# A graph attention layer on one core: ScalarE fetches rows of one tile in every 16th pair, issues the sum loads, and the last stores lose their order

## The chip, the core and the metric

The kernel runs on one core of a Trainium2 chip. The core has a matrix engine (PE in the profile; PEld are its weight loads), a vector engine (DVE), a scalar engine (ACT, called ScalarE in the text), a general engine (POOL) and a sync engine (SP) that mostly issues transfers. Each engine works through its own queue in order, and semaphores tie the queues together. Transfers run on 16 DMA engines which all queues share. SP, ScalarE and POOL can issue them; rows marked SPq, ACTq or POOLq are what these queues do themselves. The metric is device microseconds for one execution, less is better.

## The reference

A pre-norm graph layer over 12,500 nodes of 128 features and 400,000 edges that are sorted by destination (`dst`), with 32 attributes each:

```python
h = jnp.maximum(_layernorm(x, axis=-1), 0.0)
# inside the layer, on hn = ln1(h):
src = jnp.concatenate([edge_index[0], loop]); dst = jnp.concatenate([edge_index[1], loop])
ea = jnp.concatenate([edge_attr, mean of edge_attr for each self loop])
x_l = (hn @ W_l).reshape(n, H, C); x_r = (hn @ W_r).reshape(n, H, C); e = (ea @ W_e).reshape(-1, H, C)
m = jax.nn.leaky_relu(x_l[src] + x_r[dst] + e, 0.2)
alpha = jnp.einsum('ehc,hc->eh', m, att)
a = softmax of alpha over the edges of each dst
out = jax.ops.segment_sum(x_l[src] * a[:, :, None], dst, num_segments=n)
h2 = h + out + bias
result = x + h2 + gelu(ln2(h2) @ W1 + b1) @ W2 + b2
```

(The self-loop and softmax lines are told in words; H is 8 heads, C 16 features of a head, n the number of nodes.)

## The kernel before

**Start.** Nodes are padded to 98 tiles of 128. The start normalises them in quads of four tiles, multiplies by `W_l` and stores rows of 136 floats (128 products, then eight ones, which sum the weights later) in `xl_dram`; all of that must be stored before a row can be gathered from it. Meanwhile POOL gathers raw inputs for 29 pairs (`raw_gather`, L339), whose rows are later computed in the kernel instead of being gathered. Near the end of the start, at step 14, SP loads the table `hand_sb` (L841): for each tile whose rows are fetched one by one, the 128 source indices of its edges, one partition for a tile. In memory these indices lie apart, so the transfer has 4 bytes an element. At step 16 DVE multiplies them by the row size (L851), in the middle of its work on the quads.

**Pairs and rounds.** The edges form 3125 tiles of 128; four tiles are a pair (two units of two tiles), and there are 782 pairs, the last with one tile. One long loop, unrolled and ordered by hand, runs over rounds r. In each round a table of stages is gone through in order, each for the pair c = r minus its delay, and this order is the order of every engine's queue:

- `gather` (delay -4, L1078): POOL fetches each tile's 128 rows of `xl_dram` by one indirect DMA into `xs`, which has 12 buffers
- `combine` (0): PE transposes the four tiles of rows (L1143) and adds the products of destination rows and edge attributes (L1146)
- `slope` and `bend` (1): ScalarE scales (L1157), DVE takes the maximum (L1162)
- `apart`, `score` (2): PE multiplies by the attention weights (L1152, L1167)
- `lowest` (3): DVE takes minima (L1173); `weigh` (3): ScalarE's two exponentials (L1184)
- `turn` (4): PE transposes the weights (L1192); `keep_turned` (5): ScalarE copies them (L1197)
- `collect` (6): PE multiplies weights by rows (L1206); `own_heads` (7): DVE picks each head's part (L1215, L1221) into the record `rec`
- `put` (8, a late stage): SP stores the record in the `state` tensor (L1230)
- `windows` (-4, late, every fourth round): SP loads attributes, destinations and destination rows for four pairs (L1104 to L1119)

Each stage waits for stages of an earlier round on another engine, and for the `lowest`/`weigh` and `slope`/`bend` pairs in the same round. Within a round ScalarE's order is `keep_turned`, `slope`, `weigh`, then whatever else falls in the round: square roots and normalisations of node groups, which need other activation tables than the exponential (rows ACT_TABLE_LOAD).

**Rows fetched one by one.** In some pairs the fourth tile isn't gathered by POOL. `hand` issues 128 transfers of one row (544 bytes) each instead, L1056, spread over the rounds ahead, and every 16 rows it loads 16 row addresses from `hand_sb` into registers (`words`, L1010). There are two `ways`: SP does 35 pairs, from 30 in steps of 22 (last 778); ScalarE does 11 pairs, from 77 in steps of 64 (last 717), two rows a round, issued behind all other work of the round. One round before the pair comes up, the queue waits until all 128 rows have landed. The tiles have two buffers for each way.

**Stores.** The records of different pairs lie apart, so `put` may lift the order among its stores, but it does so only where `fetched` (the list of rows that SP issued in this round) isn't empty. SP issues rows up to round 771, so from pair 764 on each store waits until the one before has landed. `put` also reads the stores' addresses, four at a time (`ats`, from `at_sb`, L1010), in the round where `windows` needs them first.

**Mean of the attributes.** `sum_load` (L1248) loads 98 pieces of 512 KB, one every second round in rounds 0 to 194, on SP's queue; DVE sums them.

**Node groups.** When a group of nodes has all its records, its two states are loaded (`f_state`, L1292) and merged, normalised and passed through the feed-forward part in steps with a round each. The second last group's steps are the table `soon`, from round 774 on; the last group's (`last_steps`) come behind the last pair, in round 790 and 791, and end the kernel with the store of its output (L1545).

Of the kernel before, what the change touches and what calls it, by code (L numbers as in the profile page):

```python
# [22 lines left out]
P = 128  # L23
# [14 lines left out]
QP = 4  # L38
# [24 lines left out]
BEHIND = 3  # L63
# [9 lines left out]
HAND_LEAD = 6  # L73
HAND_READ = 16
LANDED = 7
BESIDE_EVERY = 64
BESIDE_FIRST = 77
BESIDE_LANDED = 3
# [874 lines left out]
def window_edges(  # L953
# [30 lines left out]
    with ExitStack() as es:  # L984
# [51 lines left out]

        def hand(r, w):

            w["new"].clear()
            hands, n = w["pairs"], w["sems"]  # L1040
            i, k = divmod(r + HAND_LEAD + hands.step - hands[0], hands.step)
            if k == HAND_LEAD - 1 and 0 < i <= len(hands):
                all_here = w["queue"].wait_ge(w["landed"][(i - 1) % n], ((i - 1) // n + 1) * P * 16)
                tc.declare_fence(all_here.ins, group=f"{w['name']}{i - 1}")
            if not 0 <= i < len(hands):
                return
            d = by_hand[hands[i]]
            if k == 0:
                d["x"] = once.tile([P, XW], F32, name=f"{w['name']}{i % 2}")
            for e in range(P * k // hands.step, P * (k + 1) // hands.step):  # L1050
                if e % HAND_READ == 0:
                    d["at"] = words(
                        hand_sb[w["at"] + i : w["at"] + i + 1, e : min(e + HAND_READ, P)], (NT * P - 1) * XW * 4,
                        w["engine"],
                    )
                row = w["queue"].dma_start(  # L1056
                    d["x"][e : e + 1, :].bitcast(U8), rows_at(xl_dram, d["at"][e % HAND_READ], 1, XW * 4)
                )
                row.then_inc(w["landed"][i % n], 16)
                tc.no_tile_sem_insts.add(row.ins.name)  # L1060
                tc.add_to_no_dep_group(f"{w['name']}{i}", row.ins)
                w["new"].append(row)
# [162 lines left out]
        def put(c):  # L1225
            if c % QP == 0:
                for i in range(c, min(c + QP, n_pr)):
                    pairs[i]["put"] = ats(c // QP + BEHIND)[1 + i - c]
            d, nu = pairs[c], len(tiles_of(c))
            store = nc.sync.dma_start(states_at(d["put"])[:, 0:nu], d["rec"][0 : KN * H, 0:nu].bitcast(U8))  # L1230
            if fetched:
                tc.declare_no_dep(
# [3 lines left out]
            tc.add_to_no_dep_group("states", store.ins)  # L1236
            if fetched:
                tc.declare_no_dep(
                    store.ins, group="merged",
                    reason="pairs behind a node group's round begin above its nodes, which the check of destinations asks",  # L1240
                )


        sums = [None] * NL

        def sum_load(i):
            sums[i] = fin.tile([P, LW], F32, name="ea_s", tag="big", bufs=3)
            nc.sync.dma_start(  # L1248
                sums[i],
# [294 lines left out]
        def f_put(d):  # L1544
# [15 lines left out]
            (-1, place),  # L1560
        )
        late_stages = (
            (-WAHEAD, windows),
# [43 lines left out]
            (1, f_low),  # L1607
            (2, f_exp),
            (3, f_den),
            (4, f_out),  # L1610
            (5, f_h),
            (6, f_stats),
            (7, f_root),
            (8, f_scale),
            (8, f_rest),
        )
# [63 lines left out]
        with tc.manual_schedule():  # L1680
            for r in range(-AHEAD, max(last_round, groups[-1]["round"] + 18)):
                in_round(r, early, groups[:-2])
                for late, f in stages:
                    c = r - late
                    if 0 <= c < n_pr:
                        f(c)
                for late, f in sum_stages:
                    i, off = divmod(r - late, SUM_STEP)
# [9 lines left out]
                in_round(r, enumerate(raw_steps), raw)  # L1698
                for w in ways:
                    hand(r, w)  # L1700
                t, off = divmod(r, CLEAR)
# [363 lines left out]
```

## Time and profile before

| | before |
|---|---|
| median of 3 runs | 3902.61 us (3902.32 to 3906.65) |
| profiled execution, its own time | 3904.92 us |
| span of the profiled execution | 3903.2 us |
| PE busy | 3414.5 us (87%) |
| POOL busy | 2913.6 us (75%), of it 2798.4 in 2963 gathers |
| DVE busy | 2799.8 us (72%) |
| ACT busy | 2177.5 us (56%) |
| rows fetched by SP, by ScalarE | 4480, 1408 |
| DMA traffic | 549.30 MB, 141 GB/s on the mean |

How to read a profile row: a group has its line in the kernel, its engine and operation, what it writes and reads, and how often; then busy time, mean duration in ns, and the idle time of the engine just ahead of it with what ended that idle time ("<-"). "issue" means that the engine waited for nothing that the profile shows. Timeline rows begin with the start and the duration in us, chain rows (the chain of work that ended last) likewise. Window rows have the busy time and number of instructions of PE, PEld, DVE, ACT and POOL in a stretch, then the clock granted to PE, the busy share of the DMA engines and GB/s. Rows of one line's instructions have minimum/median/maximum duration in ns, then first and last start. A query's rows are not quoted with their headings.

### The profile page before, as it was taken

Reading aid. Unit: us, or ns where it says so; the run is one execution under the profiler, and the core shown is the slowest. Engines: PE = TensorE matmul, PEld = TensorE weight load, DVE = VectorE, ACT = ScalarE, POOL = GpSimd, SP = SyncE. Lnnn points to the kernel's source line nnn. Section 1 sums busy time; section 2 is a strip of 40 time slices with the busy share of each in tenths; the row PEclk is TensorE's granted clock in tenths of the full one; section 3 lists DMA queues with packets and bytes.
Section 4 is the critical chain, followed back from the end, with each engine's and each line's share of the span. In section 5 each row is a group of like instructions: output and inputs, shape, how many; then the busy total and the mean of one; then the engine's idle time right before and its main releaser. Section 6 shows DMA issues by size and latency. Waiting matters only on the chain.

```text
span 3903.2 us, 70516 instructions
## 1 busy us (share of the span) xinstructions
PE 3414.5 (87%) x18461; PEld 2329.9 (60%) x18463; DVE 2799.8 (72%) x6142; ACT 2177.5 (56%) x4745; POOL 2913.6 (75%) x3092
## 2 busy tenths in 40 slices
PE   3588899889899989998999899999998989898988
PEld 3356566556566666665666666666666666666655
DVE  5577877777776776777777777777777767667665
ACT  6545555555565555555555555655555556456444
POOL 7777777777777777777777777777777777777773
PEclk6799999999999999999999999999999999999999
DMA  8767777777766666665565555555565555555553
GB/s 203 236 163 173 184 184 182 177 185 185 177 135 134 136 131 130 137 132 125 123 131 124 123 126 126 125 123 121 121 125 126 123 123 112 124 122 117 122 119 65
DMA packets 546765, 549.30 MB, mean 141 GB/s; under 512 B 248891, under 2 KB 425372, under 8 KB 545932
## 3 DMA queue, kind: packets, MB, share of 16 engines
q1 hardware_dynamic: 444290, 329.68, 34.3%
q0 software_dynamic: 98528, 214.12, 28.9%
q8 instruction: 150, 2.46, 0.3%
q14 instruction: 261, 2.14, 0.2%
q10 hardware_dynamic: 3536, 0.91, 0.1%
HBM read 482.08 MB, written 62.28 MB: 139 GB/s over the span
## 4 chain that ended last, share of the span: by engine, by line
PE 36%; POOL 24%; DMA 20%; issue 13%; DVE 2%; SPq 1%; ACT 0%; ACTq 0%; POOLq 0%
POOL xs L1078 24%; DMA xs<-xl_dram,src_sb 19%; PE z L1146 8%; PE acc L1206 8%; PE ab L1167 6%; PE pt_ps L1192 4%; PE z L1143 4%; PE ab L1152 2%; PE acc L1525 1%; DMA state<-rec 0%; DVE rec L1173 0%; PE acc L1500 0%; PE pt_ps L759 0%; DMA zw<-xr_dram 0%; PE acc L1328 0%
## 5 line engine op out<-in xcount | busy, mean ns | idle before, releaser
L1078 POOL DMA_INDIRECT xs<-xl_dram,src_sb x2963 | 2798.4, 944 | 904.3 <-issue 783.9
L1184 ACT ACTIVATE p<-ab,rec 128x256 f32<-128x256 f32 x1563 | 656.4, 471 | 923.6 <-DVE rec L1173 909.3
L1215 DVE TENSOR_TENSOR own<-acc,diag 128x272 f32<-128x272 f32 x782 | 342.6, 438 | 821.9 <-PE acc L1206 813.2
L1143 PE MATMUL z<-ident,xs 128*128 128x128 f32 x3079 | 564.7, 283 | 360.6 <-DMA xs<-xl_dram,src_sb 337.9
L1206 PE MATMUL acc<-xs,pt 128*128 128x136 f32 x6158 | 873.7, 286 | 0.0
L1143 PEld LDWEIGHTS z<-ident,xs 128*128 128x128 f32 x3079 | 395.3, 142 | 776.8 <-DMA xs<-xl_dram,src_sb 449.7
L1146 PE MATMUL z<-ea,zw 128*128 128x512 f32 x1564 | 828.0, 612 | 6.5 <-DMA xs<-xl_dram,src_sb 6.5
L1197 ACT COPY pt<-pt_ps 128x512 f32<-128x512 f32 x782 | 456.2, 583 | 643.6 <-PE pt_ps L1192 585.5
L1167 PE MATMUL ab<-m,negrep 128*128 128x512 f32 x1564 | 806.4, 597 | 0.2 <-issue 0.2
L1206 PEld LDWEIGHTS acc<-xs,pt 128*128 128x128 f32 x6158 | 800.7, 197 | 0.0
L1192 PEld LDWEIGHTS pt_ps<-ident,p 128*128 128x128 f32 x3125 | 408.0, 146 | 345.0 <-issue 269.7
L1162 DVE TENSOR_TENSOR m<-z,zs 128x512 f32<-128x512 f32 x782 | 533.6, 682 | 108.1 <-ACT zs L1157 106.2
L1129 DVE TENSOR_SCALAR ea<-dl,wid 96x516 f32<-96x516 bf16 x782 | 575.4, 736 | 8.0 <-DMA dl<-dc_dram 8.0
L1173 DVE TENSOR_REDUCE rec<-ab 128x2 f32<-128x512 f32 x781 | 539.0, 690 | 14.2 <-PE ab L1167 13.7
L1192 PE MATMUL pt_ps<-ident,p 128*128 128x128 f32 x3125 | 490.7, 281 | 0.6 <-ACT p L1184 0.6
L1157 ACT ACTIVATE zs<-z 128x512 f32<-128x512 f32 x782 | 471.8, 603 | 31.0 <-PE z L1146 31.0
L1221 DVE TENSOR_REDUCE rec<-own 128x34 f32<-128x272 f32 x782 | 340.9, 436 | 26.7
L1152 PE MATMUL ab<-ne,farw 128*128 128x512 bf16 (+1 forms) x781 | 306.8, 393 | 24.6 <-ACT p L1184 22.9
L1146 PEld LDWEIGHTS z<-ea,zw 128*128 128x128 f32 x1564 | 253.1, 202 | 7.3 <-issue 6.8
L1167 PEld LDWEIGHTS ab<-m,negrep 128*128 128x128 f32 x1564 | 245.8, 195 | 1.1 <-DMA ea_s<-in_ea_t 0.7
L1152 PEld LDWEIGHTS <-farw 128*128 128x128 bf16 x782 | 78.1, 100 | 211.9 <-issue 102.2
L1184 ACT ACT_TABLE_LOAD x102 | 130.9, 1283 | 1.8
(249 smaller groups left out, 2215.6 us busy)
## 6 DMA issues: line engine op xcount, KB each, us to landing
dl<-dc_dram SPq DMA_DIRECT2D x196, 396.0 KB
hand<-xl_dram SPq DMA_DIRECT2D x4480, 0.5 KB
ea<-in_ea_t SPq DMA_DIRECT2D x196, 256.0 KB
ea_s<-in_ea_t SPq DMA_DIRECT2D x98, 512.0 KB
xs<-xl_dram,src_sb POOLq DMA_INDIRECT x2963
beside<-xl_dram ACTq DMA_DIRECT2D x1408, 0.5 KB
state<-empty SPq DMA_DIRECT2D x98, 144.0 KB
f_st<-state SPq DMA_DIRECT2D x46, 288.0 KB
```

The lines of the kernel that those rows point to most:

```text
L1078: nc.gpsimd.indirect_dma_start(out=xs[:, j, :], out_offset=None, in_=xl_dram, in_offset=bass.IndirectOffsetOnAxis(ap=src_sb[:, c * KP + j ...
L1129: nc.vector.tensor_scalar(d["ea"][0:WN].rearrange("p (a b) -> p a b", b=OW), d["dl"][0:WN].rearrange("p (a b) -> p a b", b=OS)[:, :, 0:OW] ...
L1143: nc.tensor.matmul(z[:, j * P : (j + 1) * P], row_of(c, j)[:, 0:P], ident, start=(j == 0), stop=False, is_transpose=True)
L1146: nc.tensor.matmul(z[:, :e], d["zw"], d["ea"][:, :e], start=False, stop=True)
L1152: nc.tensor.matmul(d["ab"][:, :e], d["far"], d["ne"][:, :e], start=True, stop=False)
L1157: nc.scalar.activation(d["zs"][:, :e], d["z"][:, :e], AF.Copy, scale=SLOPE)
L1162: nc.vector.tensor_tensor(d["m"][:, :e], d["z"][:, :e], d["zs"][:, :e], op=OP.max)
L1167: nc.tensor.matmul(d["ab"][:, :e], negrep.rearrange("p n h -> p (n h)"), d["m"][:, :e], start=False, stop=True)
L1173: nc.vector.tensor_reduce(d["rec"][:, :, CX], d["ab"].rearrange("p (u e) -> p u e", e=U), AX.X, OP.min)
L1184: nc.scalar.activation(d["p"][:, us], d["ab"][:, us], AF.Exp, bias=d["rec"][:, i, CX:SH], scale=-1.0)
L1192: nc.tensor.transpose(d["pt_ps"][:, js], d["p"][:, js], ident)
L1206: nc.tensor.matmul(d["acc"][:, i, :], d["pt"][:, j * P : (j + 1) * P], row_of(c, j), start=(j == js[0]), stop=(j == js[-1]),)
```

## The change

Seven edits. ScalarE's tiles come in every 16th pair from 29 on (47 of them, the last in pair 765), so eight rows fall in a round. `hand` takes a share of the round's rows, and ScalarE's are issued in three places of its queue: half behind `slope`, a quarter behind `weigh`, and the last quarter behind the next round's `keep_turned` (`behind` is 1 there). SP's rows stay where they were. `put` lifts the order among stores also for pairs behind SP's last tile (779 to 781), with a wait for that tile's rows. `put` reads the addresses of the next four pairs right behind the store of the first of four. `sum_load` is issued by ScalarE. In `soon` the steps from `f_exp` on stand one to three rounds earlier.

```diff
@@ -73,8 +73,8 @@
 HAND_LEAD = 6
 HAND_READ = 16
 LANDED = 7
-BESIDE_EVERY = 64
-BESIDE_FIRST = 77
+BESIDE_EVERY = 16
+BESIDE_FIRST = 29
 BESIDE_LANDED = 3
 BESIDE_AT = 64
 BIG = 2.0**126
@@ -1034,20 +1034,23 @@
         for w in ways:
             w["landed"] = [tc.alloc_semaphore(f"{w['name']}_landed{i}") for i in range(w["sems"])]
 
-        def hand(r, w):
-
-            w["new"].clear()
+        def hand(r, w, share=(0, 1), behind=0):
+
             hands, n = w["pairs"], w["sems"]
             i, k = divmod(r + HAND_LEAD + hands.step - hands[0], hands.step)
-            if k == HAND_LEAD - 1 and 0 < i <= len(hands):
-                all_here = w["queue"].wait_ge(w["landed"][(i - 1) % n], ((i - 1) // n + 1) * P * 16)
-                tc.declare_fence(all_here.ins, group=f"{w['name']}{i - 1}")
+            if share[0] == 0:
+                w["new"].clear()
+                if k == HAND_LEAD - 1 and 0 < i <= len(hands):
+                    all_here = w["queue"].wait_ge(w["landed"][(i - 1) % n], ((i - 1) // n + 1) * P * 16)
+                    tc.declare_fence(all_here.ins, group=f"{w['name']}{i - 1}")
+            i, k = divmod(i * hands.step + k - behind, hands.step)
             if not 0 <= i < len(hands):
                 return
             d = by_hand[hands[i]]
-            if k == 0:
+            if k == 0 and share[0] == 0:
                 d["x"] = once.tile([P, XW], F32, name=f"{w['name']}{i % 2}")
-            for e in range(P * k // hands.step, P * (k + 1) // hands.step):
+            first, last = P * k // hands.step, P * (k + 1) // hands.step
+            for e in range(*(first + int((last - first) * x) for x in share)):
                 if e % HAND_READ == 0:
                     d["at"] = words(
                         hand_sb[w["at"] + i : w["at"] + i + 1, e : min(e + HAND_READ, P)], (NT * P - 1) * XW * 4,
@@ -1227,25 +1230,30 @@
                 for i in range(c, min(c + QP, n_pr)):
                     pairs[i]["put"] = ats(c // QP + BEHIND)[1 + i - c]
             d, nu = pairs[c], len(tiles_of(c))
+            free = bool(fetched) or c > hands[-1]
+            if free and not fetched:
+                nc.sync.wait_ge(ways[0]["landed"][(len(hands) - 1) % LANDED], ((len(hands) - 1) // LANDED + 1) * P * 16)
             store = nc.sync.dma_start(states_at(d["put"])[:, 0:nu], d["rec"][0 : KN * H, 0:nu].bitcast(U8))
-            if fetched:
+            if free:
                 tc.declare_no_dep(
                     store.ins, group="states",
                     reason="the nodes that pairs store lie apart, which the check of destinations asks",
                 )
             tc.add_to_no_dep_group("states", store.ins)
-            if fetched:
+            if free:
                 tc.declare_no_dep(
                     store.ins, group="merged",
                     reason="pairs behind a node group's round begin above its nodes, which the check of destinations asks",
                 )
+            if c % QP == 0 and c + QP < n_pr:
+                ats(c // QP + BEHIND + 1)
 
 
         sums = [None] * NL
 
         def sum_load(i):
             sums[i] = fin.tile([P, LW], F32, name="ea_s", tag="big", bufs=3)
-            nc.sync.dma_start(
+            nc.scalar.dma_start(
                 sums[i],
                 bass.AP(tensor=ea_t.tensor, offset=ea_t.offset + i * LW, ap=[[e_pad, DE], [EQ, QP], [1, LW]]),
             )
@@ -1559,6 +1567,7 @@
             (3, weigh),
             (-1, place),
         )
+        beside_at = {slope: ((0, 0.5),), weigh: ((0.5, 0.75),), keep_turned: ((0.75, 1), 1)}
         late_stages = (
             (-WAHEAD, windows),
             (LATE + PUT, put),
@@ -1605,14 +1614,14 @@
             (-9, f_kept),
             (0, f_state),
             (1, f_low),
-            (2, f_exp),
-            (3, f_den),
-            (4, f_out),
-            (5, f_h),
-            (6, f_stats),
-            (7, f_root),
-            (8, f_scale),
-            (8, f_rest),
+            (1, f_exp),
+            (2, f_den),
+            (2, f_out),
+            (3, f_h),
+            (3, f_stats),
+            (4, f_root),
+            (5, f_scale),
+            (5, f_rest),
         )
         after = (
             (-2, f_ready),
@@ -1684,6 +1693,8 @@
                     c = r - late
                     if 0 <= c < n_pr:
                         f(c)
+                    if f in beside_at:
+                        hand(r, ways[1], *beside_at[f])
                 for late, f in sum_stages:
                     i, off = divmod(r - late, SUM_STEP)
                     if off == 0 and 0 <= i < NL:
@@ -1696,8 +1707,7 @@
                 in_round(r, last_steps, groups[-1:])
                 in_round(r, enumerate(xr_steps), qs[1:])
                 in_round(r, enumerate(raw_steps), raw)
-                for w in ways:
-                    hand(r, w)
+                hand(r, ways[0])
                 t, off = divmod(r, CLEAR)
                 if off == 0 and CLEARED <= t + CLEARED < NT and t >= 0:
                     tc.declare_no_dep(
```

## The prediction

> **What bounds the kernel now.** I read the page first (busy times, then the costliest groups with the idle time before them), then the waits, then the timeline of single engines at the start, in the steady loop and at the end.
>
> ```profile
> span 3903.2 us, 70516 instructions
> ...
> PE 3414.5 (87%) x18461; PEld 2329.9 (60%) x18463; DVE 2799.8 (72%) x6142; ACT 2177.5 (56%) x4745; POOL 2913.6 (75%) x3092
> ...
> L1078 POOL DMA_INDIRECT xs<-xl_dram,src_sb x2963 | 2798.4, 944 | 904.3 <-issue 783.9
> L1184 ACT ACTIVATE p<-ab,rec 128x256 f32<-128x256 f32 x1563 | 656.4, 471 | 923.6 <-DVE rec L1173 909.3
> ...
> L1143 PE MATMUL z<-ident,xs 128*128 128x128 f32 x3079 | 564.7, 283 | 360.6 <-DMA xs<-xl_dram,src_sb 337.9
> ...
> L1197 ACT COPY pt<-pt_ps 128x512 f32<-128x512 f32 x782 | 456.2, 583 | 643.6 <-PE pt_ps L1192 585.5
> ...
> L1184 ACT ACT_TABLE_LOAD x102 | 130.9, 1283 | 1.8
> ```
>
> PE looks like the bound at 87%, but it waits 337.9 us for gathered rows, while POOL at 75% is never held up by another engine: the idle time before its gathers is "issue". The next rows show how such a gather is to be counted.
>
> ```profile
> POOL xs L1078 <- issue: 783.9, 2568, 1.1
> ```
>
> ```profile
> 151.88 0.94 POOL L339 DMA_INDIRECT raw<-in_x,src_raw  x1 [0.31 <-issue]
> 153.92 0.94 POOL L1078 DMA_INDIRECT xs<-xl_dram,src_sb  x1 [1.10 <-issue]
> ...
> 3854.66 0.94 POOL L1078 DMA_INDIRECT xs<-xl_dram,src_sb  x1 [0.30 <-issue]
> ```
>
> A gather is 0.94 us busy with 0.30 us behind it, and the longest such gap is 1.1 us: POOL runs from 153.92 to 3854.66 without a stop, 2962 steps of (3854.66 - 153.92) / 2962 = 1.249 us. Four gathers make a round of 5.0 us. So three parts make the span: the start up to the first gather (153.9 us), POOL's chain (3700.7 us), and the end behind the last gather (48.5 us). Can PE follow a faster POOL? When its rows are there, it can:
>
> ```profile
> 3809.40 0.60 PE L1143 MATMUL z<-ident,xs 128*128 128x128 f32 x4
> ...
> 3813.14 0.60 PE L1143 MATMUL z<-ident,xs 128*128 128x128 f32 x4
> ```
>
> From one pair's first transposes to the next pair's is 3.74 us here, against 5.0 us of POOL. Rounds with node-group work are longer, but PE then catches up by over a microsecond a round, and twelve xs buffers lie between the two.
>
> **The change part by part.** Pairs fetched by ScalarE: from 77 on in steps of 64 there are 11, from 29 on in steps of 16 up to 765 there are 47. **POOL** loses 36 gathers: 36 x 1.249 = 45.0 us from the chain that sets the time. As the PE waits above exceed this more than sevenfold, I take it whole.
>
> **ScalarE** gets 36 x 128 = 4608 more row fetches and 36 x 8 = 288 more loads of 16 row addresses. What these cost is in the trace already, at a quarter of the density:
>
> ```profile
> L1056 SPq DMA_DIRECT2D hand<-xl_dram x4480: 224/228/1467, 170.0 to 3807.4; - x195
> ...
> L1056 ACTq DMA_DIRECT2D beside<-xl_dram x1408: 227/228/684, 197.8 to 3521.1; - x176
> ```
>
> ```profile
> L1010 ACTq TENSOR_LOAD <-hand_sb x88: 1188/1199/1785, 196.5 to 3488.8; - x88
> ```
>
> ```profile
> 2019.79 0.47 ACT L1184 ACTIVATE p<-ab,rec 128x256 f32<-128x256 f32 x1 [2.23 <-DVE rec L1173]
> 2019.86 0.23 ACTq L1056 DMA_DIRECT2D beside<-xl_dram  x1
> 2020.16 0.47 ACT L1184 ACTIVATE p<-ab,rec 128x256 f32<-128x256 f32 x1
> 2020.18 0.23 ACTq L1056 DMA_DIRECT2D beside<-xl_dram  x1
> ...
> 2021.45 0.59 ACT L1197 COPY pt<-pt_ps 128x512 f32<-128x512 f32 x1
> 2021.93 0.60 ACT L1157 ACTIVATE zs<-z 128x512 f32<-128x512 f32 x1
> 2023.96 0.47 ACT L1184 ACTIVATE p<-ab,rec 128x256 f32<-128x256 f32 x1 [1.43 <-DVE rec L1173]
> ```
>
> Fetches come 0.32 us apart (2019.86, 2020.18), and both lie under the two exponentials: ScalarE's queue issues while its datapath computes. Eight a round are 2.6 us, plus half an address load, 0.6 us. Place by place: two behind the exponentials (0.64 us) lie under 0.84 us of them, cost 0. Two behind the turned copy (0.64 us) push the slope, which follows 0.48 us later now (2021.45 to 2021.93), by some 0.2 us. Four behind the slope take 1.28 us, and 2.5 us in every second round with the address load; the exponential follows 2.03 us later now, 1.43 us of it idle, so 0.5 us is left over every second round. Behind it are queued the exponentials, and for them waits PE's transpose of p, one PE round later. Together about 0.5 us a round, against (909.3 + 585.5) / 782 = 1.9 us in which ScalarE now waits for DVE and PE. I take 0; were the cover gone, see the rivals. The wait for all 128 rows stands one round ahead of the pair, five rounds behind the last fetch.
>
> **Sum loads.** 98 issues leave SP for ScalarE, one every second round up to round 194.
>
> ```profile
> L1248 SPq DMA_DIRECT2D ea_s<-in_ea_t x98: 366/442/1352, 163.1 to 1063.4; - x98
> ```
>
> At SP's 0.44 us they are 43 us, 0.2 us a round in that stretch, inside the idle time just counted. I take 0, and 0 for what SP gains, since POOL, not SP, sets the pace. The at_sb words read four pairs ahead are the same reads at another place of SP's queue: 0 too.
>
> **The start** pays. The table of row addresses is fetched as single 4-byte words, 35 x 128 = 4480 for SP and 11 x 128 = 1408 for ScalarE; now the second is 47 x 128 = 6016. DVE must multiply both before it goes on.
>
> ```profile
> 76.68 13.21 SPq L841 DMA_DIRECT2D hand_sb<-in_src  x2
> ...
> 91.15 0.22 DVE L851 TENSOR_SCALAR hand_sb<-hand_sb 35x128 int32<-35x128 int32 x1 [9.73 <-DMA hand_sb<-in_src]
> ...
> 92.93 0.37 DVE L851 TENSOR_SCALAR hand_sb<-hand_sb 11x128 int32<-11x128 int32 x1 [1.56 <-DMA hand_sb<-in_src]
> ...
> 93.77 0.72 ACT L494 ACTIVATE dlr<-df,qf 98x516 bf16<-98x516 f32 x1 [8.96 <-DVE df L480]
> ```
>
> ```profile
> DMA packets 3302, 0.37 MB, mean 93 GB/s; under 512 B 3218, under 2 KB 3218, under 8 KB 3300
> ```
>
> ```profile
> DMA packets 2785, 0.28 MB, mean 69 GB/s; under 512 B 2668, under 2 KB 2728, under 8 KB 2785
> ```
>
> ```profile
> 100.00:140.00 40.00, 20.78 (x122) 18.96 (x122) 29.85 (x179) 40.00 (x183) 30.25 (x33) 0.79 0.71 217
> ```
>
> The two DMA rows are the stretches 84 to 88 and 88 to 92 us: 3218 + 2668 small packets in 8 us, 736 a microsecond, and nearly all 5888 words. 4608 more take 6.3 us. SP's queue, DVE and behind it ScalarE (8.96 us idle) stand still for that; the window row shows ScalarE busy all of 100 to 140 us afterwards, so nothing is caught up, the last node rows are stored 6.3 us later, and POOL's first gather, whose gap of 1.10 us shows that it waited for them, starts later too. Bounds: 0 if hidden after all; from 76.68 to 91.15 for 4480 words, as if nothing else were moved, 14.9 us. I take +6.3, the measured rate.
>
> **The end.** The stores of the last 18 pairs each wait for the one before; the change frees the last three (pairs 779 to 781), and moves the second last node group up to three rounds forward.
>
> ```profile
> 3864.52 1.28 ACT L1449
> ...
> 3866.69 1.28 ACT L1184
> ...
> 3875.60 1.48 DMA state<-rec
> ...
> 3878.81 1.40 DMA state<-rec
> 3880.23 2.86 DMA f_st<-state
> ```
>
> ```profile
> 3855.83 0.38 PE L1152 MATMUL ab<-ne,farw 128*128 128x512 bf16 x1 [2.05 <-ACT p L1184]
> ...
> 3876.14 0.30 DVE L1221 TENSOR_REDUCE rec<-own 128x17 f32<-128x136 f32 x1
> ```
>
> The last record is ready at 3876.44 and could be stored at 3876.5, landing 1.40 us later at 3877.9; the load f_st starts at 3880.23 now: 2.3 us saved. The two table loads of the node group's square root (2.56 us) stand in the chain while the pipeline drains; moved to rounds with gathers still to wait for, they save perhaps 2.0 us, and the stall of 2.05 us, behind the group's products on DVE, as much again. Sum -6.3 us. Bounds: 0, and -7.8 if all of ScalarE's chain from 3864.52 to the end of its second load (3.45 us) goes.
>
> **Sum.** 3903.2 - 45.0 + 6.3 - 6.3 = 3858.2 us of span. The profiled execution took 3904.92 us, 1.7 us more than its span, and the median of the runs, 3902.61 us, lies 2.3 us below it: 3858.2 + 1.7 - 2.3 = 3857.6, rounded to 3858 us.
>
> **Rivals.** *ScalarE becomes the bound: slower.* If issuing did not overlap its work, its time would be 2177.5 + 6016 x 0.32 + 376 x 1.20 + 98 x 0.44 = 4597 us. Of the 2376 us of fetches and address loads 29% must lie under its own instructions or the kernel is slower than 3903 us. By the places above 0.84 has room for 0.64, 0.58 of 0.64 and 0.60 of 1.28 + 0.6 are covered: 1.8 of 3.2 us, 57%. Against it stands also that this row density was never run, so 0.07.
>
> *The two issuing queues exclude each other: slower.* Each ScalarE issue that meets SP's would cost SP half an issue, 0.11 us. SP issues row fetches in 4480 x 0.228 = 1021 us, 26% of the span; 4608 x 0.114 x 0.26 = 137 us, and if SP then set the rounds, 3858 + 137 = 3995 us. Against it:
>
> ```profile
> 2080.62 0.34 SPq L1119 DMA_DIRECT2D zw<-xr_dram  x1
> ...
> 2080.72 0.23 ACTq L1056 DMA_DIRECT2D beside<-xl_dram  x1
> ```
>
> The second lies inside the first, and neither is longer than when alone. 0.04. [...]
>
> *ScalarE comes late in the rounds with a table load: half the gain.* There 1.28 us stands between slope and exponential beside 2.5 us of issuing. All 102 such loads uncovered are 131 us; the PE lag that they build must exceed the reserve of xs buffers to stop POOL, so a fifth at most: 3858 + 26 = 3884 us. 0.14.
>
> *The gathers were hidden anyway:* then only start and end remain, 3903 us. That no gap on POOL is longer than 1.1 us speaks against it: 0.04.
>
> **How the numbers follow.** Forecast 0.71, rivals 0.07, 0.04, 0.14, 0.04. The forecast's own range is 3850 (start hidden, best end) to 3873 us (14.9 us at the start, no gain at the end). With 2 us below, since a profile and the runs differ by that much, and stretched to the third rival, it is 3848 to 3884, which leaves out 0.15. Less than 0.2% (8 us) cannot be told from no change here. Faster 0.71 + 0.14 = 0.85, same 0.04, slower 0.11.
>
> **What would show it.** In the profile after: 2927 gathers still 1.249 us apart with no gap from another engine; the first at about 160 us, and a second DVE wait at the address table of about 8 us; ScalarE's wait for DVE's minimum cut to a fraction of 909 us; the last state load 25.6 us behind the start of the last gather now (3854.66 to 3880.23) and some 20 us then. Wrong it would be if gaps on POOL named PE, if ScalarE's waits vanished, or if SP's issues lengthened.

## The result, and the profile after

The changed kernel takes **3937.8 us** (median of 4 runs, 3935.2 to 3941.0) against 3903.1 us (4 runs, 3902.3 to 3906.7): a ratio of 1.0088, 95% interval 1.0070 to 1.0105. It is slower, and lies 80 us above the forecast of 3858 us.

These are the lines of the changed kernel's page that answer to those shown of before:

```profile
span 3934.2 us, 80022 instructions
...
PE 3423.8 (87%) x18462; PEld 2330.2 (59%) x18463; DVE 2794.2 (71%) x6142; ACT 2188.9 (56%) x4745; POOL 2879.5 (73%) x3056
...
L1081 POOL DMA_INDIRECT xs<-xl_dram,src_sb x2927 | 2764.6, 945 | 943.7 <-issue 763.6
L1187 ACT ACTIVATE p<-ab,rec 128x256 f32<-128x256 f32 x1563 | 656.9, 472 | 1005.0 <-DVE rec L1176 428.5
...
L1165 DVE TENSOR_TENSOR m<-z,zs 128x512 f32<-128x512 f32 x782 | 535.4, 685 | 407.5 <-ACT zs L1160 396.4
```

The gathers went from 2963 to 2927, as meant, and one still takes 0.945 us. But POOL's idle time ahead of them rose from 904.3 to 943.7 us, and a new wait is large: DVE waits 396.4 us for ScalarE's slope. That sum is too large to be the loss itself; where the time went is read from POOL, which sets the pace. Its first and last gather and its waits (a row of waits has their sum in us, their number and the longest):

```profile
187.14 0.94 POOL L1081 DMA_INDIRECT xs<-xl_dram,src_sb  x1 [3.84 <-issue]
...
3890.64 0.95 POOL L1081 DMA_INDIRECT xs<-xl_dram,src_sb  x1 [0.30 <-PE pt_ps L1195]
```

```profile
POOL xs L1081 <- PE acc L1209: 68.8, 77, 4.1
```

Three terms: the first gather starts at 187.14 us instead of 153.92 (**+33.2**). From it to the last one are 3703.5 us, where 2926 steps of 1.249 us would be 3654.6: **48.9 us of gaps** (1.2 before), with up to 4.1 us behind PE. The tail behind the last gather is 3934.2 - 3890.6 = 43.6 us (48.5 before, **-4.9**). With -45.0 for 36 gathers: 33.2 + 47.7 - 4.9 - 45.0 = +31.0, the difference of the spans (3934.2 - 3903.2).

**The start.** The second table's words land at another rate. These are the packets of 84 to 88 us, then those of 100 to 108 us (108 to 116 us has the same line), SP's issues, and DVE's instruction behind them:

```profile
DMA packets 3185, 0.37 MB, mean 91 GB/s; under 512 B 3105, under 2 KB 3105, under 8 KB 3182
```

```profile
DMA packets 1360, 0.01 MB, mean 1 GB/s; under 512 B 1360, under 2 KB 1360, under 8 KB 1360
```

```profile
76.27 11.42 SPq L841 DMA_DIRECT2D hand_sb<-in_src  x2
87.79 37.33 SPq L645 DMA_DIRECT2D xl_dram<-xl  x1
```

```profile
126.05 0.22 DVE L851 TENSOR_SCALAR hand_sb<-hand_sb 47x128 int32<-47x128 int32 x1 [34.67 <-DMA hand_sb<-in_src]
```

While both tables land there are 776 small packets a microsecond; then 1360 in 8 us, 170 a microsecond, which for 6016 words is 35.4 us. SP's next issue takes 37.33 us, and DVE stands still for 34.67 us, where it stood 1.56 us for the table of 11 rows.

**The gaps.** 22 of the 23 gaps over 0.3 us lie between 560 and 1650 us. The timeline of ScalarE, and a line of SP's, around one of its waits:

```profile
604.44 0.51 ACT L1187 ACTIVATE p<-ab,rec 128x256 f32<-128x256 f32 x1
611.73 0.38 ACTq L1256 DMA_DIRECT2D ea_s<-in_ea_t  x1
612.16 0.49 ACT L729 ACTIVATE xr<-xr,l_m,l_r 128x128 f32<-128x128 f32 x1 [7.21 <-DMA zw<-xr_dram]
```

```profile
605.93 0.42 SPq L787 DMA_DIRECT2D state<-empty  x1
```

ScalarE does nothing from 604.95 us until the sum load is issued at 611.73. Sum loads and SP's transfers take their completion semaphores (counters that tell that a transfer has landed) from one set of eight in turn (in the trace each of the eight has 265 or 266 issues, sum loads and transfers of SP's mixed); the one whose turn it is was last given to the clearing of the states that SP issued at 605.93, and the sum load, with all of ScalarE's queue behind it, waits until that has landed, at 611.71 us in the trace. Over all 98 sum loads the time between the instruction ahead and the issue adds up to 149 us (waits for other events than that semaphore included), 13.4 us of it ahead of the first; ahead of every wait over 2 us the semaphore taken was last given to a transfer of SP's. The waits of 400 to 1200 us name such transfers for ScalarE, which before named none but one load of 2.0 us:

```profile
ACT L716 <- DMA ea<-in_ea_t: 21.7, 5, 5.1
ACT xr L729 <- DMA state<-rec: 20.6, 6, 6.0
...
ACT pt L1200 <- DMA state<-empty: 16.8, 4, 4.9
ACT pt L1200 <- DMA zw<-xr_dram: 15.2, 4, 5.9
```

SP has a new wait too. In the same stretch its record store waits for the clearing of the states; first before, then after:

```profile
SPq L1230 <- DMA state<-empty: 4.4, 7, 1.0
```

```profile
SPq L1236 <- DMA state<-empty: 86.6, 39, 4.7
```

Before, the reading of the stores' addresses (0.72 to 1.78 us there, median 1.52) stood between the clearing and the store in one of four rounds; the change moved it behind the store.

### The profile page after: what moved, and what is told of

The parts are those of the page before. It is cut to its first block, busy times and chain, and to the rows that moved or that the text cites. A ratio compares the mean times of both kernels' runs of the same rounds, so it can differ in the third digit from the quotient of the medians.

```text
span 3934.2 us, 80022 instructions
## 1 busy us (share of the span) xinstructions
PE 3423.8 (87%) x18462; PEld 2330.2 (59%) x18463; DVE 2794.2 (71%) x6142; ACT 2188.9 (56%) x4745; POOL 2879.5 (73%) x3056
## 4 chain that ended last, share of the span: by engine, by line
PE 29%; DMA 18%; POOL 13%; issue 10%; DVE 9%; ACTq 7%; ACT 5%; SPq 4%; POOLq 0%; DVEq 0%
POOL xs L1081 13%; DMA xs<-xl_dram,src_sb 11%; PE acc L1209 7%; PE z L1149 6%; PE ab L1170 5%; ACTq L1059 5%; PE pt_ps L1195 4%; PE z L1146 3%; DMA state<-rec 2%; SPq L1059 2%; PE ab L1155 2%; DVE m L1165 2%; DVE ea L1132 2%; DMA state<-empty 1%; DVE rec L1176 1%
## 5 line engine op out<-in xcount | busy, mean ns | idle before, releaser
L1081 POOL DMA_INDIRECT xs<-xl_dram,src_sb x2927 | 2764.6, 945 | 943.7 <-issue 763.6
L1209 PE MATMUL acc<-xs,pt 128*128 128x136 f32 x6086 | 861.9, 285 | 1.7 <-DVE f_wt L1373 1.7
L1165 DVE TENSOR_TENSOR m<-z,zs 128x512 f32<-128x512 f32 x782 | 535.4, 685 | 407.5 <-ACT zs L1160 396.4
L1209 PEld LDWEIGHTS acc<-xs,pt 128*128 128x128 f32 x6086 | 788.6, 196 | 1.9 <-DVE f_wt L1373 1.9
L1146 PEld LDWEIGHTS z<-ident,xs 128*128 128x128 f32 x3043 | 386.9, 143 | 579.0 <-DMA xs<-xl_dram,src_sb 230.3
L1146 PE MATMUL z<-ident,xs 128*128 128x128 f32 x3043 | 524.4, 281 | 191.0 <-DMA xs<-xl_dram,src_sb 168.1
L1155 PE MATMUL ab<-ne,farw 128*128 128x512 bf16 x782 | 306.0, 391 | 81.5 <-ACT p L1187 42.6
```

What stands on the lines that cost most here:

```text
L1081: nc.gpsimd.indirect_dma_start(out=xs[:, j, :], out_offset=None, in_=xl_dram, in_offset=bass.IndirectOffsetOnAxis(ap=src_sb[:, c * KP + j ...
L1146: nc.tensor.matmul(z[:, j * P : (j + 1) * P], row_of(c, j)[:, 0:P], ident, start=(j == 0), stop=False, is_transpose=True)
L1155: nc.tensor.matmul(d["ab"][:, :e], d["far"], d["ne"][:, :e], start=True, stop=False)
L1165: nc.vector.tensor_tensor(d["m"][:, :e], d["z"][:, :e], d["zs"][:, :e], op=OP.max)
L1209: nc.tensor.matmul(d["acc"][:, i, :], d["pt"][:, j * P : (j + 1) * P], row_of(c, j), start=(j == js[0]), stop=(j == js[-1]),)
```

## The experiments

Theories: A, the row count of the table sets the start; B, the sum loads hold ScalarE through the shared semaphores; C, the moved address reading holds SP. Rivals: the number of words; ScalarE's rows themselves; the ring, that is the sum loads' place among ScalarE's own transfers. Beside each group of runs the kernel before ran on the same chip, and ratios are to that. "Gaps" is, in one profile, the time from first to last gather less 1.249 us a step. The profiled execution is not always a typical one: it took 9.6 us less than the median in e3 and 14.2 less in g3, and 8.6 us more in e4 and 5.6 more in g1; elsewhere it is within 4.2 us of the median. So the ratios say what a part costs, and the gaps where.

| run | rows of the table | sum loads | address reading | ratio to before (95%) | first gather, us | gaps, us |
|---|---|---|---|---|---|---|
| the change | 47 | ScalarE | moved | 1.0088 (1.0070 to 1.0105) | 187.1 | 48.9 |
| e1 | 48 | ScalarE | moved | 1.0008 (0.9998 to 1.0017) | 156.4 | 51.5 |
| e2 | 47 | SP | moved | 1.0072 (1.0056 to 1.0089) | 185.6 | 55.0 |
| e3 | 48 | SP | moved | 0.9998 (0.9988 to 1.0007) | 157.0 | 40.3 |
| e4 | 47 | ScalarE, own semaphores | moved | 1.0016 (1.0006 to 1.0025) | 187.2 | 35.5 |
| f1 | 48 | SP | back | 0.9891 (0.9875 to 0.9908) | 155.8 | 3.8 |
| f3 | 48 | ScalarE | back | 0.9946 (0.9930 to 0.9963) | 157.1 | 26.5 |
| g2 | 48 | ScalarE, own semaphores | back | 0.9880 (0.9863 to 0.9896) | 156.5 | 2.6 |
| g1 | 48 | SP | moved, clearing behind store | 0.9967 (0.9956 to 0.9978) | 158.2 | 42.1 |
| h1 | 48 | ScalarE, own semaphores | moved, clearing behind store | 0.9916 (0.9899 to 0.9932) | 155.0 | 23.3 |
| g3 | 48 | SP | back; rows in one place | 1.0012 (0.9999 to 1.0024) | 156.8 | 39.2 |
| f4 | 48 | SP | back; end as before | 0.9906 (0.9889 to 0.9923) | 156.8 | 2.3 |
| f2 | 11 | SP | moved, nothing else | 1.0002 (0.9992 to 1.0011) | 153.5 | 0.6 |

**e1, 48 rows.** The last row is loaded and not read.

```diff
-    hand_sb = keep.tile([BESIDE_AT + len(beside), P], I32, name="hand_sb")
+    hand_sb = keep.tile([BESIDE_AT + len(beside) + 1, P], I32, name="hand_sb")
...
-                for at, h in ((0, hands), (BESIDE_AT, beside)):
+                for at, h, n in ((0, hands, len(hands)), (BESIDE_AT, beside, len(beside) + 1)):
...
-                            ap=[[h.step * UP * KU, len(h)], [NCH * K, P]],
+                            ap=[[h.step * UP * KU, n], [NCH * K, P]],
```

> The changed kernel with the second address table loaded as 48 rows instead of 47 (the 48th is never read); all else as in the changed kernel (3937.8 us, first gather at 187.1 us against 153.9 before). Theory A, the number of rows decides over how many DMA engines the 4-byte words go (the trace after shows them landing at 170 a microsecond, about one engine, where 35 and 11 rows landed at 736): the table lands in some 6 to 8 us, the first gather starts at about 157 to 160 us, and the kernel takes 3905 to 3911 us. [...] Rival, the number of words sets the time: 128 words more, first gather at 187 to 188 us, 3938 us. Both theories: the gaps on POOL between 560 and 1650 us stay, 47 us in all.

The packets of 88 to 92 us and DVE's waits at the table, with 48 rows:

```profile
DMA packets 4669, 0.24 MB, mean 59 GB/s; under 512 B 4616, under 2 KB 4616, under 8 KB 4669
```

```profile
DVE hand_sb L851 <- DMA hand_sb<-in_src: 13.7, 2, 8.9
```

The longer wait of the two is for SP's table; that for ScalarE's is 4.77 us.

A holds: more words land, at 1167 packets a microsecond while both tables are under way, and the first gather is at 156.4 us, 31 us sooner for one row more. The gaps stay.

**e2, sum loads on SP; e3, both.** Against the change, `nc.scalar.dma_start` in `sum_load` is `nc.sync.dma_start` again.

```diff
-            nc.scalar.dma_start(
+            nc.sync.dma_start(
                 sums[i],
```

> The changed kernel with the 98 sum loads issued by SP again, as before the change; rows by ScalarE, table and end as in the changed kernel. Theory B, ScalarE stands still ahead of sum loads because the completion semaphore that a sum load takes was last used by a transfer of SP that hasn't landed (149 us in all in the trace after, up to 7.2 us at a time): without them ScalarE is never blocked, the 47 us of gaps on POOL go, POOL's chain is 2926 steps of 1.249 us = 3655 us, and the kernel takes 3887 to 3893 us. Rival 1, eight rows a round with their address loads are too much for ScalarE in the rounds that also have node work (the gaps lie below round 300, where it is densest): the gaps stay, 3930 to 3938 us. Both: first gather still at 187 us.

> Both: table of 48 rows and sum loads on SP. If theories A and B hold and their gains add (30 and 47 us), 3858 to 3864 us, with the first gather at 157 to 160 us and no gap over 1.5 us on POOL. If only A holds 3908, if only B holds 3890.

B as I had put it fails: e2 takes 3938.0 us and e3 3905.7, the gaps are 55.0 and 40.3 us, and the gain of both together is that of the table alone. With the sum loads back on SP something else stops PE. SP's timeline and PE's in e3:

```profile
941.16 0.43 SPq L787 DMA_DIRECT2D state<-empty  x1
...
943.46 0.38 SPq L1122 DMA_DIRECT2D zw<-xr_dram  x1
946.45 0.35 SPq L1236 DMA_DIRECT2D state<-rec  x1
948.32 2.94 SPq L1059 DMA_DIRECT2D hand<-xl_dram  x5
```

```profile
948.25 0.47 PE L1146 MATMUL z<-ident,hand 128*128 128x128 f32 x1 [8.20 <-SPq L1044]
```

```profile
953.80 0.94 POOL L1081 DMA_INDIRECT xs<-xl_dram,src_sb  x1 [7.26 <-PE acc L1209]
```

Read from below: POOL stands for 7.26 us because PE hasn't freed a buffer; PE had stood for 8.20 us for SP's event that a tile fetched by SP has landed (L1044). SP came to that event late: its store was ready behind the load at 943.84, but was issued at 946.45, and the address reading, 1.27 us, follows it ahead of the event. PE's three longest waits of this kind (7.5, 8.2 and 8.1 us, at pairs 118, 162 and 294) lie whole multiples of 44 pairs apart, some 210 us each, where a round of loads meets a pair of SP's. Not every gap is of this kind: the one of 5.2 us that ends at 1131.9 us comes behind a load of node-group rows (`f_xl`), for which ScalarE waits 7.9 us.

**e4, own semaphores.** The sum loads stay on ScalarE, with the change's table and reading.

```diff
-            nc.scalar.dma_start(
+            load = nc.scalar.dma_start(
...
+            load.then_inc(sums_here[i % 3], 16)
+            tc.no_tile_sem_insts.add(load.ins.name)
+            tc.add_to_no_dep_group(f"sums{i}", load.ins)
...
         def sum_up(i):
+            here = nc.vector.wait_ge(sums_here[i % 3], (i // 3 + 1) * 16)
+            tc.declare_fence(here.ins, group=f"sums{i}")
```

> The changed kernel with sum loads still on ScalarE, but completing on three semaphores of their own, for which DVE waits ahead of each sum; table and all else as changed. Theory B (the wait is for SP's transfers through a shared completion semaphore): ScalarE's waits ahead of the sum loads go, and the time is that of the run with sum loads on SP, 3887 to 3895 us. Rival 2, it is the sum loads' place in ScalarE's own ring (rows fetched for the hand tiles queue behind 512 KB, or the issue itself is what delays): gaps on POOL stay, 3930 to 3938 us.

3914.2 us, 24 less than the change (28 by the ratios): about half of what was expected. The waits of ScalarE for SP's transfers are gone, SP's for the clearing are not (90 us between 400 and 1200 us), and 35.5 us of gaps are left, with PE behind SP's event ahead of most of the large ones (the largest comes behind the `f_xl` load again, for which ScalarE waits 11.8 us). So two mechanisms hold PE, and with one taken out the other still does. Beside e2, the same kernel with the sum loads on SP, e4 takes 24 us less on the same chip: with the reading moved, the sum loads cost on SP's queue too, so e2 had only changed one cost for another.

**The reading back: f1, f2, f3.** f1 is e3, f3 is e1, each without the two lines below; f2 is the kernel before with them and nothing else.

```diff
-            if c % QP == 0 and c + QP < n_pr:
-                ats(c // QP + BEHIND + 1)
```

> The kernel of the run with the addresses read back in their old place (48 rows, sum loads on SP), for a chip on which the kernel before takes about 3905 us; where it took 4956 us, SP's MOVEs ahead of a row took some 120 ns instead of 30 and the pace was not POOL's. Theory C (the moved read uncovers SP's wait for the clearing of the states): SP's waits for state<-empty below 10 us between 400 and 1200 us, no gap over 1.5 us on POOL, 3860 to 3868 us, 0.988 to 0.991 of before. Rival 1 (the added rows make all transfers land later and hold SP): waits and 20 to 35 us of gaps stay, 3885 to 3905 us. Rival 2 (ScalarE's rows too dense): gaps stay, SP's waits go.

> The kernel before with the stores' addresses read behind the store of the first of four pairs and nothing else, on such a chip. Theory C: SP's waits for state<-empty rise from 4.4 us to 40 us or more between 400 and 1200 us, gaps of 3 to 7 us stand on POOL every 44 pairs (220 us) up to about 1700 us, and the kernel takes 10 to 30 us more than before. Rivals 1 and 2: within 3 us of before.

> As the first of this call, but with the sum loads on ScalarE as in the change, on the shared completion semaphores. Theory B beside C: ScalarE is held ahead of the sum loads by SP's transfers (149 us in the trace after); what of it reaches POOL is the difference to the first: 10 to 40 us more, 3875 to 3900 us. If SP's lateness alone made the gaps: the time of the first.

These kernels and that of g2 had been run once before (as e5 to e8), on a chip on which the kernel before takes 4956 us and POOL does not set the pace (in e6, which is f2's kernel, its gathers wait 464.2 us for PE's L1206); their ratios there, 0.998 to 1.014, say nothing of the gaps. On the chip of f1 to f4 f1 takes **3860.2 us**. SP's waits of 400 to 1200 us in f1, e3 and f2, in this order:

```profile
SPq L1236 <- DMA state<-empty: 30.9, 31, 2.4
```

```profile
SPq L1236 <- DMA state<-empty: 72.3, 38, 3.5
```

```profile
SPq L1230 <- DMA state<-empty: 43.3, 30, 3.1
```

PE's waits for SP's event that a tile has landed, in f1 and e3, over the same stretch:

```profile
PE z L1146 <- SPq L1044: 12.9, 5, 5.1
```

```profile
PE z L1146 <- SPq L1044: 34.9, 8, 8.2
```

The reading alone adds 39 us to SP's wait and costs nothing (f2: the expected 10 to 30 us did not come). The rows and the rest without it add 27 us, and there is no gap to speak of (f1; the wait didn't fall below 10 us, as I had expected). Both together make 72 us and 36.5 us more gaps (40.3 against 3.8). So SP's waits add up, and the gaps don't: that is how a reserve is used up. In this stretch of f1 PE waits up to 5.1 us for SP's event without a gap on POOL: each part is hidden alone. f3 then prices the sum loads with SP out of the way: 0.9946 against 0.9891, 0.55% or 21 us. And e1 against f1 prices both parts together, 0.0117 or 46 us, about what the change's gaps are.

**g1 and h1, the clearing behind the store** (in e3, and in h1 with the semaphores of e4), and **g2**, f3 with the semaphores of e4.

```diff
                 hand(r, ways[0])
+                for late, f in late_stages:
...
                 t, off = divmod(r, CLEAR)
...
-                for late, f in late_stages:
```

> The run with both (48 rows, sum loads on SP, addresses still read behind the store), and the clearing of the states issued behind the round's store instead of ahead of its loads. Theory C, what the moved read costs is SP's wait at the store for the clearing that was issued 2.6 to 3.5 us ahead of it: now a whole round lies between the clearing and the next store, SP's waits for state<-empty fall from 72 us to under 10 us between 400 and 1200 us, the gaps on POOL (35 us) go although the read stays where the change put it, and the ratio to before is 0.988 to 0.991. Rival, the place of the read itself costs (1.2 us of SP's queue between the store and the landed event): waits for state<-empty go, the gaps stay, ratio 0.997 to 1.000.

> 48 rows, addresses read where they were, sum loads on ScalarE with three completion semaphores of their own. Theory B: what the sum loads on ScalarE cost (ratio 0.9946 against 0.9891 with them on SP) is the wait for SP's transfers behind the shared semaphores, so the ratio is 0.988 to 0.991 here too. Rival, the loads' place in ScalarE's ring, ahead of its rows: 0.994 to 0.996.

> 48 rows, sum loads on ScalarE with semaphores of their own, the clearing behind the store, the addresses read behind the store: the change with its three waits taken out and nothing of it undone. If theories A, B and C hold there is no gap on POOL, and the kernel takes the time of the run with sum loads on SP and the read back, ratio 0.987 to 0.991; if the sum loads' ring or the read's place costs by itself, 0.993 or more.

g1 did not do what it was made for: the next store, about a round later, still waits for the clearing, 39 times and up to 3.9 us, so 66 us of the wait stay, and 42.1 us of gaps in the profile. Yet it is faster than e3, 0.9967 against 0.9998, with intervals that do not meet: some 12 of the 42 us that the reading costs with the sum loads on SP go when the clearing stands elsewhere. h1 has 97 us of the wait and 23.3 us of gaps. Neither tells how much of the rest the reading costs through that wait and how much by its own 1.2 us in SP's queue, ahead of the event. g2 is clear: with own semaphores the sum loads on ScalarE cost nothing, **3858.1 us**, ratio 0.9880; POOL has no gap over 0.5 us, and the rival, their place in ScalarE's ring, falls. DVE's waits for ScalarE's slope show the same, f3 first, then g2 (400 to 1200 us):

```profile
DVE m L1165 <- ACT zs L1160: 162.3, 96, 7.3
```

```profile
DVE m L1165 <- ACT zs L1160: 31.6, 36, 6.0
```

SP's waits for the clearing are 56.3 us in g2, against 72.3 in e3, and there is no gap: their sum alone doesn't decide. PE's waits for SP's event, 7.2 us, stay small.

ScalarE's largest waits of 400 to 1200 us in g2 name DVE and PE again; the only wait for a transfer over 1 us is one of 7.2 us for a load of node-group rows:

```profile
ACT p L1187 <- DVE rec L1176: 111.7, 67, 7.8
ACT p L1187 <- DVE m L1165: 77.7, 42, 2.5
ACT pt L1200 <- PE pt_ps L1195: 41.1, 44, 5.7
```

**g3, rows in one place.** f1 with ScalarE's eight rows issued together at the end of the round.

```diff
-        beside_at = {slope: ((0, 0.5),), weigh: ((0.5, 0.75),), keep_turned: ((0.75, 1), 1)}
...
-                    if f in beside_at:
-                        hand(r, ways[1], *beside_at[f])
...
-                hand(r, ways[0])
+                for w in ways:
+                    hand(r, w)
```

> 48 rows, sum loads on SP, addresses read where they were, but ScalarE's eight rows all at the end of the round, where its two rows stood before the change. Theory, ScalarE's queue has 1.9 us of idle time a round and eight rows are 2.6 us: in one place they delay the next round's copy and slope, DVE's wait for the slope (25 us between 400 and 1200 us) rises and gaps appear on POOL, 5 to 30 us more than with three places, ratio 0.990 to 0.997. Rival, the place doesn't matter as long as no other wait stands in the queue: within 3 us, 0.989.

47 us more than f1 by the ratios (1.0012 against 0.9891; its ten runs spread from 3896 to 3919 us), above the 5 to 30 expected, and POOL's gaps are back behind PE. DVE's waits in g3, over the whole span:

```profile
DVE m L1165 <- ACT zs L1160: 799.6, 468, 5.8
```

It was 219.7 us in f1 and 106.2 in the kernel before. In one place the rows, 2.6 us a round, hold the slope up so far that POOL stands; in three they hold it up less, and no gap comes of it.

**f4, the end.** f1 without the freed last stores and with the second last node group's steps as before.

```diff
-            free = bool(fetched) or c > hands[-1]
...
-            if free:
+            if fetched:
...
-            (1, f_exp),
...
+            (2, f_exp),
...
```

> The kernel before with ScalarE's rows in every 16th pair and in three places, and 48 rows of the table; sum loads on SP, addresses read where they were, order among the last stores and the node group's steps as before. Against the first of this call it lacks the end's two edits, which the prediction put at -6.3 us (bounds 0 and -7.8): the tail behind the last gather is 48 to 49 us against 42.5, and the kernel takes 5 to 7 us more, 3865 to 3874 us.

The tail is 46.1 us against 42.5, and the medians differ by 3.7 us with overlapping intervals: less than the 5 to 7 expected.

**Two runs on a chip with another pace: i1 and h3.** In i1 (e3 with the store freed from the last clearing, so that only the one before it is waited for) the price of C's wait was to be seen; in h3 (f1) the table is loaded as 46 rows and one.

```diff
+                tc.declare_no_dep(
+                    store.ins, group=f"clear{t}",
...
+                    tc.add_to_no_dep_group(f"clear{t}", cleared.ins)
```

> The run with both (48 rows, sum loads on SP, addresses read behind the store), and a store no longer waits for the last clearing of the states, only for the one before it (the pairs stored then lie below the tile cleared last). Moving the clearing behind the store had not taken the wait away (66 us left between 400 and 1200 us), so that run told nothing of its price. Theory C, the moved read costs through SP's wait at the store: with that wait gone (under 5 us between 400 and 1200 us) PE no longer waits for SP's landed events (36 us now), POOL's gaps (35 us) go, and the ratio to before is 0.987 to 0.991. Rival, the read's own place costs: the waits for the clearing go, gaps of 20 us or more stay, ratio 0.994 to 1.000.

> The run with the read back (sum loads on SP), with the table loaded as 46 rows and one row by itself instead of 48: a dose of the start. [...]

On this chip the kernel before takes 4948 us, so i1's ratio of 1.0168 says nothing of C, and its question stays open; nor does h3's ratio, 1.0196, say anything of the start. The start of h3 can be read, beside that of i1 (48 rows) from the same chip. Packets of 116 to 120 us in h3, and DVE's waits at the table in h3, then in i1:

```profile
DMA packets 1360, 0.01 MB, mean 1 GB/s; under 512 B 1360, under 2 KB 1360, under 8 KB 1360
```

```profile
DVE hand_sb L853 <- DMA hand_sb<-in_src: 26.8, 2, 18.0
```

```profile
DVE hand_sb L851 <- DMA hand_sb<-in_src: 13.2, 2, 8.7
```

With 46 rows 1360 packets take 4 us, not 8: 340 a microsecond, twice the rate of 47. The wait for ScalarE's table is the longer one, 18.0 us, in h3; in i1 it is the shorter, 4.5 us. That is 13.5 us more, and the first gather comes at 208.7 us, 9.2 later than i1's 199.5. So the row count sets the table's time here too, as A has it. I had expected 12 to 16 us, an estimate from twice the 170 of 47 rows: the rate came out so, and the delay lies below it.

## Why the prediction was wrong, step by step

- **POOL's chain, -45.0: right.** Steps of 1.249 us hold: f1 and g2, without the three costs below, run 2926 of them in 3658.4 and 3657.1 us, gaps of 3.8 and 2.6 us included, and show the gain. That g2 takes 3858.1 us, the forecast to a tenth, is luck in the small terms: in its profile the start costs 2.5 us and not 6.3, the end gains 4.6 and not 6.3, and the gaps grow by 1.4.
- **ScalarE's rows, 0: right as placed.** In three places they leave no gap (f1, g2); g3 shows that this step had 47 us at stake, and that "room" in a queue is a matter of place.
- **"Sum loads ... I take 0": the first step that failed.** It costed 98 issues by their duration, 43 us, and asked whether ScalarE had idle time for them. It did not ask what an issue may have to wait for, nor what is queued behind it: up to 7 us at a time for a transfer of SP's, 149 us ahead of the sum loads in all. Worth 0.55% (f3 against f1).
- **"The at_sb words read four pairs ahead are the same reads at another place of SP's queue: 0 too": the second.** The reason given, that POOL and not SP sets the pace, holds only while SP keeps its reserve. Beside the added rows it costs 0.0107 of the time with the sum loads on SP (e3 against f1), 0.0062 with them on ScalarE (e1 against f3); by itself nothing (f2). The two steps together cost 46 us (e1 against f1). Whether the reading costs through the wait for the clearing alone is not shown; part of it goes with the place of the clearing (g1).
- **"4608 more words take 6.3 us": the third.** Right in its place and in what stands still for it, mis-sized: +33.2 us, outside the bounds of 0 to 14.9. The rate of 736 words a microsecond was measured on tables of 35 and 11 rows and carried over to one of 47; both bounds came from the same two transfers, so the range could not see it. Alone, 47 rows land at 170 packets a microsecond (100 to 108 us) and 46 rows, on another chip, at 340 (116 to 120 us in h3); the packets' time is 9.6% and 19.1% of that of 16 DMA engines (1.5 and 3.1 of them). With 48 rows it is 1167 while both tables are under way; for 35 and 11 rows no run has a rate of each alone. Which property of the row count sets the rate, and how many DMA engines serve such a transfer, is not shown.
- **The end, -6.3 (0 to -7.8): right in kind,** 48.5 to 43.6 us, -4.9 (between f4 and f1 3.6); the last state load is issued 20.4 us behind the last gather (3910.99 us), as foreseen.
- **The rivals.** Of the signs of being wrong one came: gaps on POOL name PE. ScalarE did not become the bound, and the two issuing queues do not shut each other out, with four times the rows by ScalarE (medians of 228 ns, as before):

```profile
L1059 ACTq DMA_DIRECT2D beside<-xl_dram x6016: 227/228/861, 230.5 to 3788.8; - x195
...
L1059 SPq DMA_DIRECT2D hand<-xl_dram x4480: 224/228/655, 203.7 to 3843.0; - x195
```

The nearest rival was ScalarE late in some rounds; its mechanism, uncovered table loads, is not what the runs show. What was missing was a rival in which a queue waits for another queue's transfer.
- **Sum of the misses** in the span: start 33.2 - 6.3 = 26.9, gaps 47.8 (3703.5 against 3700.7 - 45.0), tail 43.6 - 42.2 = 1.4, together 76.0 = 3934.2 - 3858.2 (the figures are rounded).

## What to carry to other kernels

Before a transfer moves to a compute engine's queue, ask what its issue can wait for (completion semaphores shared with another queue's transfers count) and what stands behind it; give it semaphores of its own. A rate measured on one transfer need not hold for another shape (here 170, 340 and 1167 packets a microsecond with 47, 46 and 48 rows): measure it at the row count meant before costing a longer table. A part that is free by itself can cost 40 us (1% here) beside another that draws on the same reserve, so undo parts in pairs, not only one at a time.

## What the runs showed that I had not expected

One row more made a transfer of 47 x 128 single words faster: SP's next issue took 37.33 us behind 47 rows and 3.75 us behind 48. And on two of the five chips of the experiments the kernel before takes 27% more (4956 and 4948 us). On the first of the two the register moves of SP ahead of a row last up to 1397 ns in f2's kernel (e6), at a median of 29 ns, where 38 ns was the most in the profile of the kernel before, its median 29 too:

```profile
L1056 SPq MOVE hand<-xl_dram x4480: 2/29/1397, 211.0 to 4853.7; - x195
```

The 120 ns in f1's expectation stand in no row here. Why these chips take longer is open.
